# Preparing five Mambas' rates during attention, and moving small weight operations to ScalarE and GpSimd

## The chip, the cores and the metric

The kernel runs on one core of a Trainium2 chip, in one launch. The metric is the device time of that core in microseconds (us), the median of the runs shown; smaller is better.

## The reference, cut to what matters

Four layers work on an image `x` of 2 x 64 x 96 x 96 (batch, channels, height, width) in float32. Layer 0 is self-attention over the 9216 pixels of each image. Layer 1 is a depthwise and a pointwise convolution, then a Mamba over the pixels as one sequence. Layer 2 holds four Mambas: two (forward and backward) along one image axis, a linear map over both, then two along the other axis and a second linear map. Layer 3 makes a 3 x 3 filter from channel means and applies it. A Mamba, cut to its core:

```python
xz = einsum('nld,ed->nle', u, in_proj_w); x, z = split(xz, 2)
x = silu(conv1d(x, conv_w, causal, D_CONV=4) + conv_b)
dt, B, C = split(einsum('nld,ed->nle', x, x_proj_w), [4, 4 + 16])
dt = softplus(dt @ dt_proj_w.T + dt_proj_b)
A = -exp(A_log)                       # 128 channels x 16 states
h = exp(dt * A) * h + dt * B * x      # for each channel and state, step by step
y = (sum over states of h * C + x * Dp) * silu(z)
out = y @ out_proj_w.T
```

In layer 2 the input of each Mamba is normalised with a weight `norm_w`. What depends on the weights alone (A, the products of projections, repeats of rows for the layout) is worked out on the chip once for each Mamba; the change is about that preparation.

## The kernel before, in words

All of `x` stays in SBUF (`xa`, `xb`, 128 partitions: two images of 64 channels). Each engine takes its instructions in the order in which the program issues them; within the attention and the Mamba part that order is written out by hand.

**Attention** (`layer0_direct`). For each image b there are 18 blocks of 512 queries; each block has 18 steps n. A step issues eight score matmuls in 64-row pieces (L299), two exponentials (L313, ScalarE), two additions into a running sum (L402 and L411, VectorE) and the value matmuls of the step before (L324). At step 3 of a block the sums of the last block are made by a matmul into PSUM bank "m" (`sums`, L346) and inverted on VectorE (`invert`, L351 to L354). In image 0 each step ends with `next(ready_weights, None)`: one piece of the generator `prepare` (L1226), from one `yield` to the next. Its products also go to bank "m", of which there is one. `prepare` makes the tables, then everything of Mamba 0, in 16 pieces.

**Weights of a Mamba** (`mamba_weights`, L643). For Mamba i: A = -exp(A_log) (L649, L650); two products with the table `member` put A into place (L652) and a matmul turns that into `rates` (L658, copied at L661); for i > 0, `in_w` is multiplied by `norm_w` (L664); for each of four taps a matmul spreads the tap and a product with `in_w` stores it (L669, L671); then `low` (L675, L677), `step` (L679, L682), `direct`, the identity times D (L684), and in `by_state` (L631) four copies that repeat the rows of B and C (L639).

**Mamba part** (`layers1_2`, class `Mamba`). The work is cut into 120 units of 16 scan steps: 24 units of Mamba 0, whose scan state is carried on from unit to unit, then 96 units of Mambas 1 to 4, of whole sequences. A scan step is a decay on ScalarE (L973, exp), the input product `dt*x*B` on VectorE (L986), the scan on VectorE (L995 carried, L1000 whole), the product with C on GpSimd (L1002) and the gathering matmuls (L1013). The tables CARRY and FRESH give every event of a unit its due time in steps; `run` sorts all events of all units by time and issues them so. Most matmuls of this part, such as projections and weight products, share one double PSUM bank, "m".

The weights of Mambas 1 to 4 come in through the generator `other()`: two events of each carried unit, and two of each second whole unit, take one piece of it (`other_0`, `other_1`; due at 2.87 and 3.25, or at 0.72 and 0.40, steps after the unit begins). A product is issued in the first of two such pieces and read in the second. Such a pair is called a slot below. `other()` first finishes the pointwise convolution (7 slots), then takes for each of Mambas 1 and 2 7 slots, 4 for `joined` (L1276 on: the output weights multiplied with the linear map, with a fold of the identity's two halves at L1292), and the same for Mambas 3 and 4. The weights live in a part of `xa` handed out by a `Carver`; its first tiles are the scratch `placed` and the repeats of Mamba 0, made at the start of `layers1_2` on VectorE.

Of the kernel before, what the change touches and what calls it, by code (L numbers as in the profile page):

```python
# [25 lines left out]
P = 128  # L26
B, C, H, W = 2, 64, 96, 96
# [4 lines left out]
D_STATE, DT_RANK, D_CONV = 16, 4, 4  # L32
# [3 lines left out]
NMAMBA = 5  # L36


SPAN, BLOCKS, PARTS = 16, 8, 2
GROUP = P // SPAN  # L40
# [32 lines left out]
def rows_of(b):  # L73
    return slice(b * C, (b + 1) * C)
# [490 lines left out]
def products(nc, p, lhsT, rhs, m, n):  # L565

    each = lhsT if isinstance(lhsT, list) else [lhsT]
    for j, one in enumerate(each):
        nc.tensor.matmul(p[:m, j * n : (j + 1) * n], lhsT=one, rhs=rhs, start=True, stop=True)
    return p[:m, : len(each) * n]  # L570
# [25 lines left out]
def mamba_tables(k, pool):  # L596

    nc = k.nc  # L600
    t = SimpleNamespace()

    t.member = pool.tile([P, SPAN], FP, name="member")
    nc.vector.reduce_sum(t.member, k.ident.rearrange("p (b i) -> p i b", i=SPAN), axis=AX.X)
    t.block = pool.tile([P, 2, BLOCKS // 2], FP, name="block")
    for z in range(2):
        own = k.ident.rearrange("p (x z i) -> p z x i", z=2, i=SPAN)[:, z]
        nc.vector.reduce_sum(t.block[:, z], own, axis=AX.X)
    t.block = t.block.rearrange("p z x -> p (z x)")

    held = pool.tile([P, 3 * SPAN], FP, name="held")
    nc.vector.memset(held, 0.0)
    own = k.ident.rearrange("p (i g) -> p i g", g=GROUP)
    nc.vector.reduce_sum(held[:, SPAN : 2 * SPAN], own, axis=AX.X)
    t.gather = [held[:, SPAN:], held[:, :TILE]]

    t.centre = pool.tile([P, 2, C], FP, name="centre")
    for j in range(2):
        nc.vector.tensor_add(t.centre[:, j], k.ident[:, :C], k.ident[:, C:])
        nc.vector.tensor_scalar_add(t.centre[:, j], t.centre[:, j], -1.0 / C)  # L620
    t.centre = t.centre.rearrange("p j c -> p (j c)")
    return t


def scratch(k, t, pool):


    t.placed = pool.tile([P, PARTS, SPAN, GROUP], FP, name="placed")


def by_state(k, w, pool, i):  # L631

    x_w = k.mat(f"x_w{i}")
    w.bc = []
    for at in (DT_RANK, DT_RANK + D_STATE):
        bc = pool.tile([P, PARTS, SPAN, GROUP], FP, name=f"bc{i}_{at}")
        for j in range(PARTS):
            own = x_w[:, at + j * GROUP : at + (j + 1) * GROUP]
            k.nc.vector.tensor_copy(bc[:, j], own.unsqueeze(1).to_broadcast([P, SPAN, GROUP]))  # L639
        w.bc.append([bc[:, j].rearrange("p i g -> p (i g)") for j in range(PARTS)])  # L640


def mamba_weights(k, w, pool, product, tables, i):  # L643

    nc = k.nc
    a = pool.tile([P, D_STATE], FP, name=f"A{i}")
    nc.scalar.activation(a, k.col(f"A_log{i}"), AF.Exp)  # L649
    nc.vector.tensor_scalar_mul(a, a, -1.0)  # L650
    for j in range(PARTS):
        nc.vector.tensor_mul(  # L652
            tables.placed[:, j],
            tables.member.unsqueeze(2).to_broadcast([P, SPAN, GROUP]),
            a[:, j * GROUP : (j + 1) * GROUP].unsqueeze(1).to_broadcast([P, SPAN, GROUP]),
        )
    placed = [tables.placed[:, j].rearrange("p i g -> p (i g)") for j in range(PARTS)]
    p = product(placed, tables.block, P, BLOCKS)  # L658
    yield
    w.rates = pool.tile([P, PARTS, BLOCKS], FP, name=f"rates{i}")  # L660
    nc.vector.tensor_copy(w.rates.rearrange("p k b -> p (k b)"), p)  # L661
    in_w = k.mat(f"in_w{i}")
    if i:
        nc.vector.tensor_scalar_mul(in_w, in_w, k.col(f"norm_w{i}"))  # L664
    yield
    conv_w = k.col(f"convd_w{i}")
    w.taps = pool.tile([P, D_CONV, P], FP, name=f"taps{i}")
    for j in range(D_CONV):
        p = product(conv_w[:, j : j + 1].to_broadcast([P, P]), k.ident, P, P)  # L669
        yield  # L670
        nc.vector.tensor_mul(w.taps[:, j], in_w[:, :P], p)  # L671
        yield
    x_w = k.mat(f"x_w{i}")
    low = pool.tile([DT_RANK, P], FP, name=f"low{i}")
    p = product(x_w[:, :DT_RANK], k.ident, DT_RANK, P)  # L675
    yield
    nc.vector.tensor_copy(low, p)  # L677
    yield
    p = product(low, k.dtw(i), P, P)  # L679
    yield  # L680
    w.step = pool.tile([P, P], FP, name=f"step{i}")
    nc.vector.tensor_copy(w.step, p)  # L682
    w.direct = pool.tile([P, P], FP, name=f"direct{i}")
    nc.vector.tensor_scalar_mul(w.direct, k.ident, k.col(f"Dp{i}"))  # L684
    if i:
        by_state(k, w, pool, i)
    w.gate_w = in_w[:, P:]
    w.conv_b, w.dt_b = k.col(f"convd_b{i}"), k.col(f"dt_b{i}")
    w.out_w = k.mat(f"out_w{i}")
    yield  # L690


class Mamba:
# [35 lines left out]
    def product(self, lhsT, rhs, m, n):  # L729
        return products(self.nc, self.ps_m.tile([P, 2 * NB], FP, tag="m", name="mm"), lhsT, rhs, m, n)  # L730
# [495 lines left out]
def prepare(k, scratch_tile, product):  # L1226


    k.tables = mamba_tables(k, k.const)
    yield  # L1230
    scratch(k, k.tables, Carver(scratch_tile))
    yield
    k.weights = [SimpleNamespace() for _ in range(NMAMBA)]
    yield from mamba_weights(k, k.weights[0], k.const, product, k.tables, 0)


def layers1_2(k, pre, padded):
# [3 lines left out]
    nc, tc = k.nc, k.tc  # L1241
# [8 lines left out]
    with ExitStack() as stack:  # L1250
        m = Mamba(k, k.tables, *[stack.enter_context(p) for p in pools])
# [12 lines left out]


        carver = Carver(k.xa)
        scratch(k, k.tables, carver)
        by_state(k, k.weights[0], carver, 0)
        dtw = carver.tile([DT_RANK, (NMAMBA - 1) * P], FP)
        nc.sync.dma_start(out=dtw, in_=k.dtw_in[:, P:])  # L1270
        k.dtw = lambda i: dtw[:, bass.ts(i - 1, P)]

        def joined(which, lin_w, to):

            p = m.ps_m.tile([P, 2 * NB], FP, tag="m", name="mm")
            for d in range(2):
                lhsT = k.mat(f"out_w{which[d]}")
                nc.tensor.matmul(p[rows_of(d), :P], lhsT=lhsT, rhs=k.ident, start=True, stop=True)  # L1280
            yield
            turned = carver.tile([P, P], FP)
            nc.vector.tensor_copy(turned, p[:, :P])
            yield
            for d in range(2):
                p = m.product(turned[rows_of(d)], k.mat(lin_w, rows_of(d)), P, C)
                yield
                nc.vector.tensor_copy(to[d], p)
                yield
            fold = carver.tile([P, 2, C], FP)  # L1290
            for d in range(2):
                nc.vector.tensor_add(fold[:, d], k.ident[:, :C], k.ident[:, C:])  # L1292
            p = m.product(fold.rearrange("p a c -> p (a c)"), k.mat(lin_w), P, C)
            yield
            nc.vector.tensor_add(to[2], fold[:, 0], p)
            yield
# [6 lines left out]
        def other():  # L1303
            for c in range(FIRST, L // CH):
                part = k.xb[:, bass.ts(c, CH)]
                sides, whole = m.open()
                for j, p in enumerate(sides):
                    rhs = part[:, bass.ts(j, HALF)]
                    nc.tensor.matmul(p, lhsT=k.mat("conv_w"), rhs=rhs, start=True, stop=True)
                yield  # L1310
                nc.scalar.activation(part, whole, AF.Relu, bias=pre.bias, scale=pre.scale)
                yield
            for (which, lin_w, _), to in zip(layer2, joins):
                for i in which:
                    yield from mamba_weights(k, k.weights[i], carver, m.product, k.tables, i)
                yield from joined(which, lin_w, to)

        units = []
# [15 lines left out]
        for (which, _, lin_b), to, order in zip(layer2, joins, ("p (t n) -> p n t", "p (n t) -> p n t")):  # L1334
            xs = k.xb.rearrange(order, n=W)
            for b in range(B):
                rows = rows_of(b)
                for n in range(0, W, SEQS):
# [13 lines left out]
                    pair[1].last, norm.unit = pair, pair[0]  # L1352
                    units += pair
        m.run(units, first, FIRST, other(), padded.early)


# [134 lines left out]
@with_exitstack  # L1491
def conv_seq_kernel(ctx: ExitStack, tc: tile.TileContext, x, cols, mats, dtw, out):
    k = setup(ctx, tc, x, cols, mats, dtw)
    dram = ctx.enter_context(tc.tile_pool(name="dram", bufs=1, space=bass.MemoryType.DRAM))
    pre = Pre(k, dram)
    layer0(k, x, pre)
    padded = Padded(k)
    with tc.manual_schedule():
        layers1_2(k, pre, padded)
        layer3(k, padded, out)  # L1500
# [81 lines left out]
```

## Time and profile before

| what | us |
|---|---|
| median of 3 runs | 7395.57 (7389.34 to 7396.07) |
| profiled execution, its own time | 7391.99 |
| its span | 7389.9 |
| busy: TensorE, VectorE, ScalarE, GpSimd | 6327.8, 6725.5, 5478.5, 4613.1 |
| end of attention (VectorE writes `bad`) | 2389.6 |
| first scan of the Mamba part, last scan's end | 2452.2, 7332.3 |

The span is the time from the first to the last instruction in the profile; the rest of the execution's own time lies around it. Busy time is that of the engine's own work: waits don't count. TensorE's span of 2.4 ms at the beginning is attention, the rest mainly the 120 units.

### The profile page before, as it was taken

Reading aid. Unit: us, or ns where it says so; the run is one execution under the profiler, and the core shown is the slowest. Engines: PE = TensorE matmul, PEld = TensorE weight load, DVE = VectorE, ACT = ScalarE, POOL = GpSimd, SP = SyncE. Lnnn points to the kernel's source line nnn. Section 1 sums busy time; section 2 is a strip of 40 time slices with the busy share of each in tenths; the row PEclk is TensorE's granted clock in tenths of the full one; section 3 lists DMA queues with packets and bytes.
Section 4 is the critical chain, followed back from the end, with each engine's and each line's share of the span. In section 5 each row is a group of like instructions: output and inputs, shape, how many; then the busy total and the mean of one; then the engine's idle time right before and its main releaser. Section 6 shows DMA issues by size and latency. Waiting matters only on the chain. (4 is left out here: it accounts for less than half of the span.)

```text
span 7389.9 us, 106037 instructions
## 1 busy us (share of the span) xinstructions
PE 6327.8 (86%) x38502; PEld 2353.7 (32%) x38502; DVE 6725.5 (91%) x5732; ACT 5478.5 (74%) x7876; POOL 4613.1 (62%) x3074
## 2 busy tenths in 40 slices
PE   9999999999999788787788788788787777777777
PEld 3333333333333333222233233233233333333333
DVE  6787887888887599999999999999999999999999
ACT  5555555555555688787888888888888888888884
POOL 0000000000000498888899899999999999999996
PEclk9999999999999799998999999999999999999998
DMA  1000000000000466666667667667767676676764
GB/s 47 1 1 1 1 1 1 3 6 6 6 6 15 123 171 158 160 164 158 172 178 185 172 175 186 177 175 183 184 175 186 178 182 181 181 183 176 187 180 129
DMA packets 301155, 878.09 MB, mean 119 GB/s; under 512 B 33608, under 2 KB 35660, under 8 KB 300112
## 3 DMA queue, kind: packets, MB, share of 16 engines
q1 hardware_dynamic: 300184, 869.94, 45.3%
q8 instruction: 303, 4.96, 0.3%
q14 instruction: 228, 1.87, 0.1%
q10 hardware_dynamic: 440, 1.32, 0.1%
HBM read 767.71 MB, written 103.42 MB: 118 GB/s over the span
## 5 line engine op out<-in xcount | busy, mean ns | idle before, releaser
L1002 POOL TENSOR_TENSOR h<-h,C 128x768 f32<-128x768 f32 x1920 | 3457.0, 1821 | 308.8 <-DVE h L1000 257.2
L1000 DVE TENSOR_TENSOR_SCAN h<-h,place 128x768 f32<-128x768 f32 x1344 | 2285.9, 1736 | 13.3 <-ACT place L973 0.5
L313 ACT ACTIVATE e<-f_exp 128x1024 f32<-128x1024 f32 x1296 | 1258.0, 1022 | 986.5 <-PE f_exp L299 986.5
L986 DVE TENSOR_TENSOR place<-spread,B 128x768 f32<-128x768 f32 x1704 | 1545.4, 946 | 130.5 <-PE B L978 90.5
L973 ACT ACTIVATE h<-spread,xa 128x384 f32<-128x384 f32 x2688 | 1445.9, 605 | 8.5 <-DMA spread<-rows 7.1
L1013 PE MATMUL y<-h,held 128*32 128x384 f32 x7680 | 1105.5, 515 | 372.0 <-POOL h L1002 371.2
L324 PE MATMUL y<-e,xb 64*64 64x512 f32 x10368 | 1232.1, 590 | 0.0
L299 PE MATMUL f_exp<-theta,phi 64*64 64x512 f32 x10368 | 1230.0, 589 | 2.0 <-DVE xb L284 1.4
L402 DVE TENSOR_TENSOR acc_e<-acc_e,e 128x1024 f32<-128x1024 f32 x612 | 771.4, 1260 | 301.1 <-ACT e L313 283.4
L338 POOL TENSOR_TENSOR ys<-ys,y_one 128x512 f32<-128x512 f32 x36 | 46.0, 1277 | 1455.0 <-DVE ys L337 1455.0
L411 DVE TENSOR_TENSOR acc_e<-acc_e,e 128x1024 f32<-128x1024 f32 x612 | 811.0, 1325 | 65.9 <-DVE acc_e L402 2.8
L978 PE MATMUL B<-raw,xa 128*128 128x384 f32 x960 | 492.5, 598 | 269.9 <-DVE place L986 267.2
L995 DVE TENSOR_TENSOR_SCAN h<-h,state,place 128x384 f32<-128x384 f32 x720 | 670.6, 990 | 2.4
L324 PEld LDWEIGHTS y<-e,xb 64*64 64x64 f32 x10368 | 393.6, 133 | 728.1 <-issue 722.4
L299 PEld LDWEIGHTS f_exp<-theta,phi 64*64 64x64 f32 x10368 | 395.5, 133 | 715.0 <-issue 703.0
L1013 PEld LDWEIGHTS y<-h,held 128*32 128x32 f32 x7680 | 212.2, 109 | 1140.8 <-POOL h L1002 741.5
L363 POOL TENSOR_TENSOR xa<-xa,t_att 64x512 f32<-64x512 f32 x36 | 54.9, 1526 | 756.6 <-ACT t_att L361 736.0
L743 PE MATMUL mm<-dtu,ident 128*128 128x384 f32 x960 | 426.8, 550 | 26.8 <-ACT xb L1051 17.4
L920 PE MATMUL mm<-raw,xa 128*128 128x384 f32 x960 | 376.9, 516 | 29.9 <-ACT xn L781 27.0
L986 POOL TENSOR_TENSOR bx<-spread,xa 128x768 f32<-128x768 f32 x216 | 393.0, 1819 | 5.5 <-ACT xa L982 3.5
L973 ACT ACTIVATE h<-spread,rates 128x384 f32<-128x384 f32 x720 | 393.1, 606 | 3.5 <-DMA spread<-rows 2.9
L978 PEld LDWEIGHTS B<-raw,xa 128*128 128x128 f32 x960 | 159.4, 208 | 585.7 <-DVE place L986 419.2
(229 smaller groups left out, 7416.8 us busy)
## 6 DMA issues: line engine op xcount, KB each, us to landing
spread<-rows SPq DMA_DIRECT2D x1920, 384.0 KB, 6.1
rows<-dtu SPq DMA_DIRECT2D x120, 768.0 KB, 4.6
image<-pre SPq DMA_DIRECT2D x11, 384.0 KB, 2.3
xb<-image SPq DMA_DIRECT2D x11, 384.0 KB, 7.1
xa<-in_x SPq DMA_DIRECT2D x1, 2304.0 KB, 22.2
xa<-in_x SPq DMA_DIRECT2D x3, 384.0 KB, 11.6
xb<-in_x SPq DMA_DIRECT2D x3, 384.0 KB, 12.4
xa<-in_x SPq DMA_DIRECT2D x1, 1152.0 KB, 18.7
```

The lines of the kernel that those rows point to most:

```text
L299: nc.tensor.matmul(f[rows_of(half), bass.ts(side, NB)], lhsT=phi[at, m * P + half * C : m * P + (half + 1) * C], rhs=theta[at, bass.ts(i, ...
L313: nc.scalar.activation(e, f, AF.Exp)
L324: nc.tensor.matmul(ys[half][rows_of(side)], lhsT=g[at, m, :], rhs=e[at, bass.ts(side, NB)], start=m < 2, stop=m >= KEYS - 2,)
L402: nc.vector.tensor_add(block.acc, block.acc, es[0])
L411: nc.vector.tensor_add(block.acc, block.acc, es[1])
L973: self.nc.scalar.activation(u.decay[step][:, q], dt[:, q], AF.Exp, scale=rate)
L978: self.nc.tensor.matmul(self.B, lhsT=u.w.bc[0][part], rhs=x, start=True, stop=True)
L986: engine.tensor_mul(u.bx[step], self.spread(u, step, 1), B)
L995: nc.vector.tensor_tensor_scan(h[:, q], decay[:, q], bx[:, q], state[:, q : q + 1], ALU.mult, ALU.add)
L1000: nc.vector.tensor_tensor_scan(*flat, 0.0, ALU.mult, ALU.add)
L1002: nc.gpsimd.tensor_mul(h, h, C)
L1013: self.nc.tensor.matmul(y, lhsT=self.t.gather[block // 4], rhs=u.h[step][:, q], start=False, stop=stop)
```

## The change

It has five parts.

1. `mamba_weights` is split. A new `mamba_rates` holds A, the placing products, `rates` and the scaling of `in_w` by `norm_w`. `prepare` calls it for all five Mambas, in attention, before the rest of Mamba 0's weights; it has one `yield` more, between the placing products and their matmul. The pieces of `prepare` go from 16 to 26.
2. Taps are made two to a product: two matmuls into one PSUM tile, then two multiplications, so two slots a Mamba in place of four.
3. The repeats of B and C go from VectorE to ScalarE, and `by_state` yields after each pair of copies, so for Mambas 1 to 4 they have a slot of their own after `step`. For Mamba 0 all four are issued at the start of `layers1_2`.
4. `direct` goes from VectorE to ScalarE.
5. The two fold sums of `joined` go from VectorE to GpSimd.

The scratch `placed` is no longer carved from `xa` in `layers1_2`. A Mamba takes 5 slots of `other()` in place of 7.

```diff
@@ by_state
-            k.nc.vector.tensor_copy(bc[:, j], own.unsqueeze(1).to_broadcast([P, SPAN, GROUP]))
+            k.nc.scalar.copy(bc[:, j], own.unsqueeze(1).to_broadcast([P, SPAN, GROUP]))
         w.bc.append([bc[:, j].rearrange("p i g -> p (i g)") for j in range(PARTS)])
-def mamba_weights(k, w, pool, product, tables, i):
+        yield
+def mamba_rates(k, w, pool, product, tables, i):
...
     placed = [tables.placed[:, j].rearrange("p i g -> p (i g)") for j in range(PARTS)]
+    yield
     p = product(placed, tables.block, P, BLOCKS)
     yield
     w.rates = pool.tile([P, PARTS, BLOCKS], FP, name=f"rates{i}")
     nc.vector.tensor_copy(w.rates.rearrange("p k b -> p (k b)"), p)
-    in_w = k.mat(f"in_w{i}")
     if i:
+        in_w = k.mat(f"in_w{i}")
         nc.vector.tensor_scalar_mul(in_w, in_w, k.col(f"norm_w{i}"))
     yield
+def mamba_weights(k, w, pool, product, i):
+    nc = k.nc
+    in_w = k.mat(f"in_w{i}")
     conv_w = k.col(f"convd_w{i}")
     w.taps = pool.tile([P, D_CONV, P], FP, name=f"taps{i}")
-    for j in range(D_CONV):
-        p = product(conv_w[:, j : j + 1].to_broadcast([P, P]), k.ident, P, P)
+    for j in range(0, D_CONV, 2):
+        p = product([conv_w[:, j + n : j + n + 1].to_broadcast([P, P]) for n in range(2)], k.ident, P, P)
         yield
-        nc.vector.tensor_mul(w.taps[:, j], in_w[:, :P], p)
+        for n in range(2):
+            nc.vector.tensor_mul(w.taps[:, j + n], in_w[:, :P], p[:, bass.ts(n, P)])
         yield
...
-    nc.vector.tensor_scalar_mul(w.direct, k.ident, k.col(f"Dp{i}"))
-    if i:
-        by_state(k, w, pool, i)
+    nc.scalar.mul(w.direct, k.ident, k.col(f"Dp{i}"))
...
     yield
+    if i:
+        yield from by_state(k, w, pool, i)
@@ prepare
-    yield from mamba_weights(k, k.weights[0], k.const, product, k.tables, 0)
+    for i in range(NMAMBA):
+        yield from mamba_rates(k, k.weights[i], k.const, product, k.tables, i)
+    yield from mamba_weights(k, k.weights[0], k.const, product, 0)
@@ layers1_2
-        scratch(k, k.tables, carver)
-        by_state(k, k.weights[0], carver, 0)
+        for _ in by_state(k, k.weights[0], carver, 0):
+            pass
...
-                nc.vector.tensor_add(fold[:, d], k.ident[:, :C], k.ident[:, C:])
+                nc.gpsimd.tensor_add(fold[:, d], k.ident[:, :C], k.ident[:, C:])
...
-                    yield from mamba_weights(k, k.weights[i], carver, m.product, k.tables, i)
+                    yield from mamba_weights(k, k.weights[i], carver, m.product, i)
```

## The prediction

> **What bounds the kernel now.** I read the page first, then the busy time of engines by windows, the timelines of VectorE and TensorE around the edited lines, and last the groups of instructions.
>
> ```profile
> PE 6327.8 (86%) x38502; PEld 2353.7 (32%) x38502; DVE 6725.5 (91%) x5732; ACT 5478.5 (74%) x7876; POOL 4613.1 (62%) x3074
> DVE  6787887888887599999999999999999999999999
> ```
>
> The kernel has two regimes. Up to about 2394 us it is attention, where TensorE works without gaps and VectorE has room. From 2452 us to 7332 us the 120 Mamba units run and VectorE is full. Busy time by windows inside that part:
>
> ```profile
> core 0: us, PE busy (x) PEld busy (x) DVE busy (x) ACT busy (x) POOL busy (x), PEclk, DMA share, GB/s
> 2661.00:2745.00 84.00, 70.89 (x290) 25.92 (x290) 83.79 (x95) 72.38 (x112) 76.33 (x75) 0.96 0.66 169
> 5451.00:5765.00 314.00, 249.11 (x1062) 97.24 (x1058) 309.43 (x241) 268.94 (x428) 291.98 (x173) 0.96 0.70 181
> ```
>
> VectorE is idle 0.2 of 84 us and 4.6 of 314 us, ScalarE 14% in both: a microsecond taken from VectorE here should come off the span. Now VectorE where a weight step falls (columns: start, time of the row, engine, line, operation, count, idle time before and what ended it):
>
> ```profile
> 2792.35 1.92 DVE L995 TENSOR_TENSOR_SCAN h<-h,state,place 128x384 f32<-128x384 f32 x2
> 2795.72 0.18 DVE L650 TENSOR_SCALAR xa<-xa 128x16 f32<-128x16 f32 x1 [1.45 <-ACT xa L649]
> 2795.93 2.11 DVE L652 TENSOR_TENSOR xa<-member,xa 128x128 f32<-128x128 f32 x2
> 2798.73 0.17 DVE L661 COPY xa<-mm 128x16 f32<-128x16 f32 x1 [0.69 <-PE mm L569]
> 2798.82 1.03 DVE L664 TENSOR_SCALAR mats<-mats,cols 128x256 f32<-128x256 f32 x1
> 2799.78 1.91 DVE L995 TENSOR_TENSOR_SCAN h<-place,state,bx 128x384 f32<-128x384 f32 x2
> ...
> 3057.44 0.29 DVE L682 COPY xa<-mm 128x128 f32<-128x128 f32 x1 [0.52 <-PE mm L569]
> 3057.65 0.94 DVE L684 TENSOR_SCALAR xa<-ident,cols 128x128 f32<-128x128 f32 x1
> 3058.52 3.88 DVE L639 COPY xa<-mats 128x128 f32<-128x128 f32 x4
> 3062.31 1.91 DVE L995 TENSOR_TENSOR_SCAN h<-place,state,bx 128x384 f32<-128x384 f32 x2
> ```
>
> The scans stand still from 2794.2 to 2799.8 for the rates and from 3056.9 to 3062.3 for step, direct and repeats: 5.5 us each time, though the operations are tiny. The four copies of L639 take 0.21 us when nothing is in the way and up to 1.85, the length of one GpSimd product (L1002, 1.82).
>
> **What the Trainium skill says.** "SBUF — State Buffer", Who interferes with whom: a VectorE copy or tensor_scalar in a two-port mode, or a product of two SBUF inputs, and a GpSimd operation hold one port pair as a lock for the whole instruction, and ScalarE never waits for it. The spread of L639, L652 and L684 fits; the ScalarE half is not tested by any row here. "Perfetto Trace Analysis", Optimizing Scalar/DVE Operations: with VectorE saturated, moving work to ScalarE may pay, to GpSimd perhaps not, because of that pair. For prices, "ScalarE: Activation LUTs", What ACT_TABLE_LOAD costs: 186 ns + 0.833 per element, 93 more for a pointer operand.
>
> **The change in the Mamba part.** From the starts of the first scan of each unit in VectorE's timeline I take unit lengths. In the first 24 units (scans carried on) an undisturbed one, units 4 to 6, takes 42.12 us; from unit 60 on a pair takes 38.79 + 39.68 = 78.47. Whatever is above is what the weight slots cost, whatever engine makes it.
>
> Carried part, units 7 to 22, excess in order: rates 5.64; four tap slots 1.23, 1.81, 0.50, 0.48; low 0.29; step with direct and repeats 5.49. Second Mamba: 5.63; 1.40, 0.49, 0.49, 0.50; 0.28; 5.50. Join: 2.50, 0.38. Sum 32.6. After it:
> - No rates slot. Two tap slots, each with two products (0.85 instead of 0.49 us of TensorE by L569) and two L671 (0.29 more): 0.5 + 0.35 + 0.29, so 1.1 each.
> - low 0.3. Step keeps its L682 alone: 0.5. Two slots of two repeats on ScalarE: 2 x 0.29 by the page's price; bounded by the 0.20 of L649 (16 wide) and 0.48 of L1017 (384 wide). `direct`, with a pointer, 0.39. All queue in ScalarE ahead of decays that are needed two to three steps (about 8 us) later; cover is ScalarE's 14% idle. I count 0.3 per Mamba; without cover it would be 1.5.
> - That is 3.3 per Mamba, 6.6 for two.
> - The join moves up into units 17 to 20: 1.5, 0.4, 0.4 and the fold slot. There GpSimd's sums (0.28 each: L1002 is 1.82 at 768 wide, the least L342 1.26 at 512, so 2.2 ns per element and 0.14) stand behind state copy 0.19 and product 1.81 of the scan just done; TensorE's product (0.65), with the matmuls queued behind it, and VectorE's add (0.22), with the next scan behind it, wait: 3.4 in all, from 2.5 if GpSimd is early to 6 if it lags.
> - Taps of the third Mamba, units 21 and 22: 2.6.
>
> Sum 14.9: **17.7 saved**. The slot at the end of unit 23 is 3542.11 to 3546.44, a fold with its lock; afterwards a step copy of 0.8: **3.5 saved**.
>
> Free part, units 24 to 59: 1434.5 us against 18 x 78.47 = 1412.5, so 22.0 above, almost all in two rates slots, two repeats slots with the pair after, and the fold of unit 59 (2.4). After it: passage into this part 1.0, repeats 0.3, two tap slots 0.6 each (single ones were hidden in the 0.9 us that odd units idle anyway), the rest of Mamba 4 0.2, join -0.5, fold 2.7 (as in the timeline at 4978 us, where GpSimd ends the previous product only at 4980.0). Sum 4.9: **17.1 saved**. Mamba part: 38.3, between 28 and 45 as slots recover less or more.
>
> **The change in attention.** Every added matmul lies on the full engine. TensorE, then VectorE of the second block:
>
> ```profile
> 49.28 0.61 PE L569 MATMUL m<-block,scratch 128*128 128x8 f32 x4 [2.19 <-DVE scratch L652]
> 56.85 0.49 PE L569 MATMUL m<-ident,cols 128*128 128x128 f32 x2
> ...
> 116.86 1.13 PE L346 MATMUL m<-fold,ones 128*128 128x512 f32 x2
> 117.92 1.95 PE L324 MATMUL y<-e,xb 64*64 64x512 f32 x16
> ...
> 119.67 3.35 DVE L351 RECIPROCAL inv<-m 128x512 f32<-128x512 f32 x1
> 124.45 0.69 DVE L354 SCALAR_TENSOR_TENSOR ok<-m,ok 128x512 f32<-128x512 f32 x1
> ```
>
> Rates now yield between L652 and the product, so the 2.2 wait goes; four more products of 0.55 come: +2.2 - 2.3 = -0.1. VectorE's added 0.7 to 1.0 per rates fits its 0.7 to 1.5 of idle per step. But preparation grows from 16 steps to 26, past the block's 18. Counting them, the product of `low` falls on step 3 of the second block, right behind `sums`, and needs the same PSUM bank "m", which VectorE reads until L354 ends at 125.1, now about 126.3. TensorE, in order, would reach it at about 120.6: **5.7 lost**, with all scores behind it. `sums` itself waits 0.4 for the tap products. Attention +6.0; if VectorE catches up sooner +3, if each rates product stalls too +10.
>
> At the passage the four repeats of Mamba 0 go to ScalarE, which idles 10.43 us before L208 at 2400.70; they start when depthwise has freed `xa` (2398.9) and take 1.2: nothing, up to 1 us if they are dearer. No DMA is moved; SP keeps its order.
>
> Sum: 6.0 - 38.3 = -32.3. The profiled execution has 7392.0 (span 7389.9 and 2.1 around it), so 7359.7. The median of the runs shown is 3.6 higher; I say 7361.
>
> **Rivals.** (1) As above, 7361, chance 0.76. (2) VectorE's time is given back in the free part: GpSimd is busy 292 of 314 there and may be the next limit, so only the carried part and unit 23 pay: 7392.0 + 6.0 - 21.2 = 7377. For it: taps in the free part already cost nothing. Against: the stops there show in the units' lengths. Chance 0.10. (3) Slower: the free part's units alternate 38.79 and 39.7, and the 0.8 us of the odd ones ends on ScalarE's copy of B (L982), so ScalarE is just in time at the unit's edge. If the moved work leaves it late for good and both units take 39.7, all 48 pairs pay 0.9: +43 - 32 = +11, 7403. It decides from 0.7 us per pair. Against it: after every disturbance (units 38, 52, 84) the old rhythm comes back within a pair or two, and the moved work is over by unit 45. Chance 0.07. (4) Attention at +10, both folds at 6 us and half the free gain: 7392.0 + 10 - (38.3 - 6 - 8.5) = 7378, 7382 on the footing of the median, which is within 0.2% (15 us, about what a measurement of this kernel can tell from no change). Chance 0.07.
>
> Range 7348 to 7378: the low end takes 45 saved and attention at +3 or so, the high end rival 2. Chances: faster 0.86, same 0.07, slower 0.07.
>
> **What would show it.** Right: L650 to L664 only before 110 us and at 0.17 to 0.35 each; no VectorE row for the repeats, `direct` or the fold; units 7 to 22 near 43 us, none at 47; one TensorE wait of 5 to 6 us near 121 us; the last scan about 32 us earlier. Wrong: unit lengths from unit 60 on other than 78.47 per pair, ScalarE repeats above 0.5 us, or a fold slot of over 6 us.

## The result, and the profile after

The changed kernel takes 7365.94 us (median of 6 runs, 7363.2 to 7369.59), against 7395.82 (6 runs, 7389.34 to 7400.15) before: 29.9 us less, a ratio of 0.996 with a 95% interval of 0.9948 to 0.9973. The forecast was 7361, 34.6 under the median that it stood on. The profiled execution took 7363.2 with a span of 7361.4, which is 28.5 under the span before; the working had said 32.3.

The page of the changed kernel, its busy times and VectorE's row over the span:

```profile
PE 6309.5 (86%) x38502; PEld 2346.8 (32%) x38502; DVE 6694.1 (91%) x5703; ACT 5493.7 (75%) x7902; POOL 4609.6 (63%) x3078
DVE  6878777888888499999999999999999999999999
```

VectorE lost 31.4 us of busy time and 29 instructions, ScalarE gained 15.2, and the span fell by nearly what VectorE lost. Busy time by windows, in the same two places of the Mamba part as before:

```profile
core 0: us, PE busy (x) PEld busy (x) DVE busy (x) ACT busy (x) POOL busy (x), PEclk, DMA share, GB/s
2669.00:2753.00 84.00, 70.56 (x290) 25.66 (x288) 83.79 (x95) 72.26 (x113) 76.25 (x75) 0.96 0.66 168
5423.00:5737.00 314.00, 249.15 (x1060) 96.88 (x1056) 309.53 (x241) 269.60 (x428) 291.84 (x173) 0.96 0.70 181
```

Where no weights are prepared nothing changed: VectorE is as full, and the other engines stand to it as before. The difference must lie in the slots and in attention. The slot with `step`, on VectorE's timeline, which before had stopped the scans for 5.5 us:

```profile
2929.29 1.92 DVE L1005 TENSOR_TENSOR_SCAN h<-h,state,place 128x384 f32<-128x384 f32 x2
2931.38 0.29 DVE L692 COPY xa<-mm 128x128 f32<-128x128 f32 x1 [0.18 <-PE mm L569]
2931.59 1.92 DVE L1005 TENSOR_TENSOR_SCAN h<-place,state,bx 128x384 f32<-128x384 f32 x2
```

The scan before it ends at 2931.2 (the row begins at 2929.29 and lasts 1.92) and the next begins at 2931.6: 0.4 us are left of 5.5. The rows of the moved operations, by their lines (count, then least, median and longest duration in ns, then the first and last start):

```profile
L650 DVE TENSOR_SCALAR A<-A x5: 168/169/171, 47.9 to 91.3; 128x16 f32<-128x16 f32 x5
L665 DVE TENSOR_SCALAR mats<-mats,cols x4: 345/345/347, 65.9 to 98.9; 128x256 f32<-128x256 f32 x4
L639 ACT COPY xa<-mats x20: 284/296/299, 2400.1 to 4008.5; 128x128 f32<-128x128 f32 x20
L694 ACT ACTIVATE xa<-ident,cols x4: 390/390/393, 2932.4 to 3929.5; 128x128 f32<-128x128 f32 x4
```

All five Mambas' rates are done by 99.3 us, and both of these VectorE operations run at their bare length, with no spread. On ScalarE every one of the twenty repeats takes 0.28 to 0.30, every `direct` 0.39: no spread, where VectorE's copies had gone from 0.21 to 1.85, and near the 0.29 and 0.39 that the working had priced them at.

The price in attention, on TensorE's timeline of the second block:

```profile
115.84 1.95 PE L324 MATMUL y<-e,xb 64*64 64x512 f32 x16
123.12 0.59 PE L569 MATMUL m<-ident,mats 128*4 128x128 f32 x2 [5.33 <-DVE ok L354]
123.64 3.35 PE L299 MATMUL f_exp<-theta,phi 64*64 64x512 f32 x16
126.82 1.89 PE L324 MATMUL y<-e,xb 64*64 64x512 f32 x16
```

TensorE stands for 5.3 us behind the inversion, as forecast. What the forecast did not have is the next row: sixteen score matmuls that take 1.90 elsewhere take 3.35. Busy time by windows shows a lower granted clock over the same time (it follows the busy times):

```profile
110.00:120.00 10.00, 7.79 (x66) 2.30 (x58) 9.10 (x8) 3.88 (x4) 0.40 (x1) 1.00 0.00 0
120.00:125.00 5.00, 1.88 (x10) 0.65 (x14) 2.93 (x4) 0.00 (x0) 0.00 (x0) 0.81 0.01 3
125.00:130.00 5.00, 5.00 (x44) 1.64 (x40) 2.64 (x3) 2.41 (x3) 0.00 (x0) 0.85 0.00 0
130.00:140.00 10.00, 10.00 (x84) 3.17 (x80) 6.51 (x7) 6.42 (x8) 0.24 (x1) 1.00 0.01 2
```

The clock falls with the pause and is back a few microseconds later.

For all that follows, the span is cut into stages by starts of rows in the timelines: attention from the first score matmul to the flag `bad`; the passage from there to the first scan; then the units by the starts of their first scans. Units 7 to 22 hold the weight slots of the carried part, 25 to 59 those of the free part. "From sums to sums" is the time from the second block's `sums` matmul to the third's. "The fold unit" is the one whose slot makes the fold sums: in the changed kernel unit 20 of the carried part, and unit 43, taken with its neighbour 44, in the free part. Each experiment was timed once, the two kernels of the last one five times; every row of the table is one profile.

| kernel | attention | sums to sums | units 0-6 | 7-22 | 23-24 | 25-59 | 60-119 |
|---|---|---|---|---|---|---|---|
| before | 2352.8 | 64.2 | 335.5 | 706.5 | 92.0 | 1394.7 | 2351.5 |
| changed | 2359.6 | 72.2 | 333.8 | 694.3 | 89.3 | 1376.0 | 2351.0 |
| again | 2360.6 | 73.5 | 333.9 | 690.5 | 89.4 | 1375.6 | 2351.6 |
| undo_rates | 2349.1 | 64.2 | 336.6 | 705.3 | 90.9 | 1379.8 | 2351.6 |
| undo_repeats | 2359.6 | 72.2 | 336.6 | 702.5 | 87.1 | 1383.9 | 2350.7 |
| undo_fold | 2360.6 | 73.4 | 336.4 | 688.7 | 84.1 | 1376.0 | 2351.6 |
| undo_taps | 2359.4 | 72.0 | 335.7 | 685.2 | 91.3 | 1374.8 | 2352.4 |
| fix_bank | 2351.7 | 65.2 | 339.5 | 696.6 | 84.1 | 1375.9 | 2351.6 |
| fold_table | 2360.6 | 73.4 | 336.1 | 688.4 | 88.5 | 1371.9 | 2351.7 |
| pad_slots | 2359.4 | 72.0 | 336.2 | 685.0 | 87.8 | 1375.0 | 2352.4 |
| all_three | 2352.6 | 65.2 | 333.3 | 686.5 | 90.7 | 1372.5 | 2351.2 |
| fix_fold_pad | 2352.0 | 65.2 | 335.6 | 685.9 | 90.7 | 1372.4 | 2351.5 |

From before to changed: attention +6.9 in itself, the start and the passage +0.7, units 0 to 6 -1.7, 7 to 22 -12.2, 23 and 24 -2.7, 25 to 59 -18.7, the rest -0.7; with these roundings -28.4 of the span's -28.5.

### The profile page after: what moved, and what is told of

Same layout as the page of the kernel before. It is cut to its first block, busy times and chain, and to the rows that moved or that the text cites. A ratio compares the mean times of both kernels' runs of the same rounds, so it can differ in the third digit from the quotient of the medians.

```text
span 7361.4 us, 106021 instructions
## 1 busy us (share of the span) xinstructions
PE 6309.5 (86%) x38502; PEld 2346.8 (32%) x38502; DVE 6694.1 (91%) x5703; ACT 5493.7 (75%) x7902; POOL 4609.6 (63%) x3078
## 4 chain that ended last, share of the span: by engine, by line
DVE 16%; issue 13%; PE 11%; ACT 6%; POOL 4%; DMA 2%; DVEq 0%; POOLq 0%; SPq 0%; ACTq 0%
DVE h L1010 9%; DVE place L996 7%; PE mm L753 6%; POOL h L1012 3%; DMA spread<-rows 2%; ACT h L983 2%; PE conv L855 2%; PE y L1023 1%; PE B L988 1%; PE y L1018 1%; ACT raw L860 1%; ACT raw L866 0%; DVE done L1483 0%; ACT xa L817 0%; ACT raw L869 0%
## 5 line engine op out<-in xcount | busy, mean ns | idle before, releaser
L1012 POOL TENSOR_TENSOR h<-h,C 128x768 f32<-128x768 f32 x1920 | 3454.1, 1819 | 291.0 <-DVE h L1010 240.7
L983 ACT ACTIVATE h<-spread,rates 128x384 f32<-128x384 f32 x3408 | 1845.3, 608 | 8.6 <-DMA spread<-rows 6.9
L299 PEld LDWEIGHTS f_exp<-theta,phi 64*64 64x64 f32 x10368 | 395.5, 133 | 714.6 <-issue 702.5
L930 PE MATMUL mm<-raw,xa 128*128 128x384 f32 x960 | 380.0, 520 | 29.9 <-ACT xn L791 27.6
L1010 DVE TENSOR_TENSOR_SCAN h<-place,bx 128x768 f32<-128x768 f32 x192 | 334.0, 1739 | 0.3 <-ACT place L983 0.3
```

Source lines behind the costliest of these rows:

```text
L299: nc.tensor.matmul(f[rows_of(half), bass.ts(side, NB)], lhsT=phi[at, m * P + half * C : m * P + (half + 1) * C], rhs=theta[at, bass.ts(i, ...
L983: self.nc.scalar.activation(u.decay[step][:, q], dt[:, q], AF.Exp, scale=rate)
L1010: nc.vector.tensor_tensor_scan(*flat, 0.0, ALU.mult, ALU.add)
L1012: nc.gpsimd.tensor_mul(h, h, C)
```

## The experiments

My theory: in the Mamba part VectorE sets the pace, and a slot costs the time for which it stops VectorE, whichever engine makes it wait; moving an operation pays where it shortens that stop. The rival readings were that the number of slots is what counts, that GpSimd takes back what VectorE gains, and that an offload helps whatever it is waited for by. Each experiment starts from the changed kernel.

**The same kernel again.** No edit.

> The changed kernel once more, to see how much of a difference between two profiles is the kernel's and how much the execution's. If the units' lengths are as fixed as the free part's rhythm suggests, the fold unit is 47.3 us again, the carried units 7 to 22 sum to 694 within 1 us, and the span from the first scan to the last is within 2 us of 4844. If executions differ in how TensorE and ScalarE stand to VectorE, the units after a tap slot (8, 9, 13) move by a microsecond and the sum by 3 to 5. The wait for bank m is 5.3 us again, and the matmuls behind it run at a lower clock for some 2 to 3 us, as in the four runs with it so far.

It took 7365.15. The carried fold unit is 47.8 (47.3 in the first profile), the Mamba part from first scan to last 4841.0 against 4844.4. The difference sits in single units with tap slots or just after them: unit 8 is 43.0 in place of 44.3, unit 9 42.4 for 43.7, unit 13 43.1 for 44.3, and unit 10 43.9 for 42.6. So the second reading held: two profiles of one kernel differ by 3.8 us in units 7 to 22, and smaller differences there say nothing. Units 4 to 6, ahead of every weight slot, repeat to 0.02 us; late in the free part single ones differ by up to 0.8.

**Rates back in the Mamba part.**

```diff
-    for i in range(NMAMBA):
-        yield from mamba_rates(k, k.weights[i], k.const, product, k.tables, i)
+    yield from mamba_rates(k, k.weights[0], k.const, product, k.tables, 0)
...
+                    yield from mamba_rates(k, k.weights[i], k.const, m.product, k.tables, i)
                     yield from mamba_weights(k, k.weights[i], carver, m.product, i)
```

> The changed kernel with the rates and the norm scaling of Mambas 1 to 4 put back into the Mamba part (one more slot each, as before the change); only Mamba 0's stay in attention. My theory (VectorE bounds the Mamba part, and a rates slot stops its scans for some 5.5 us): attention ends 7.5 us earlier than in the changed kernel (four products of 0.55 go, and the wait for bank m of 5.3 goes since preparation ends inside the first block); two carried units grow to 47.7 us (+11); two free pairs grow by 4 to 6 (+9); the third Mamba's taps move into the free part (-4). In all +8 to +9. Rival (the gain came from having fewer slots, or VectorE's time is given back in the free part): the units stay near 43 and 78.5 a pair, and the kernel is 5 to 8 us faster than the changed one.

The `yield` that the change added stays for Mamba 0 alone, and the scratch `placed` is carved in `layers1_2` again. It took 7373.61; the span is 10.1 longer than the changed kernel's. Units 7 and 13, with the rates, are 47.73 us each, and units 7 to 22 are 11.0 longer; the third Mamba's rates fall into unit 23 (51.3 for 46.8), the fourth's into unit 33 (44.1 for 39.2), and units 25 to 59 are 3.8 longer; attention is 10.5 shorter, where 7.5 had been said. That the folds move too, to units 22 (48.1) and 51 (42.0), makes the sum less clean than its parts. The rival, 5 to 8 us faster, is out: the rates slots cost VectorE 5.6 us each in the carried part. From first scan to last this kernel takes 19.8 us more than the changed one, of the 35.8 by which the change shortened that part; but 10.5 of them come back in attention, so that moving the rates is worth about 10 of the 28.5 us of the span, less than the repeats below.

**Repeats and direct back on VectorE.**

```diff
-            k.nc.scalar.copy(bc[:, j], own.unsqueeze(1).to_broadcast([P, SPAN, GROUP]))
+            k.nc.vector.tensor_copy(bc[:, j], own.unsqueeze(1).to_broadcast([P, SPAN, GROUP]))
...
-    nc.scalar.mul(w.direct, k.ident, k.col(f"Dp{i}"))
+    nc.vector.tensor_scalar_mul(w.direct, k.ident, k.col(f"Dp{i}"))
```

> The changed kernel with the repeats of B and C and direct back on VectorE, slots unchanged. My theory (VectorE is full and these operations stand behind GpSimd's hold on the shared port pair): each of the copies takes 0.2 or about 1.85 us, direct 0.9 to 1.3; a carried Mamba costs about 5 us more, a free one 2.5: +15 in all. Rival (the engine does not matter, only that the copies have a slot of their own): less than +3.

It took 7379.82, 14 more than the changed kernel (span 16.6 more). The rows of the repeats, and a slot of them on the timelines of VectorE and GpSimd in this kernel (rows between left out):

```profile
L639 DVE COPY xa<-mats x20: 213/220/1850, 2404.6 to 4026.3; 128x128 f32<-128x128 f32 x20
```

```profile
2973.82 1.92 DVE L1005 TENSOR_TENSOR_SCAN h<-h,state,place 128x384 f32<-128x384 f32 x2
2975.52 1.81 POOL L1012 TENSOR_TENSOR h<-h,C 128x768 f32<-128x768 f32 x1
2975.65 3.79 DVE L639 COPY xa<-mats 128x128 f32<-128x128 f32 x4
2977.54 1.82 POOL L1012 TENSOR_TENSOR h<-h,C 128x768 f32<-128x768 f32 x1
2979.36 1.91 DVE L1005 TENSOR_TENSOR_SCAN h<-place,state,bx 128x384 f32<-128x384 f32 x2
```

Four copies of 0.21 us by their least length hold VectorE for 3.8 between two scans, and the whole unit (number 11) is 45.86 where the changed kernel has 42.14. Units 7 to 22 are 8.2 longer, 25 to 59 7.9. The same work on ScalarE costs nothing that the units show. The theory held in mechanism: eight of the twenty copies are long (1.76 to 1.85), and each of the eight ends 0.08 to 0.09 us after a product of GpSimd, here after the ends of L1012 at 2977.3 and 2979.4. In size it held for the carried Mambas (about 5 us each); the two free ones cost 4.0 each where 2.5 was expected. The port pair that the Trainium skill's "SBUF — State Buffer" (Who interferes with whom) describes fits the two lengths, 0.21 and 1.85, and ScalarE's single one of 0.28 to 0.30 fits its sentence that ScalarE doesn't wait there.

**Fold sums back on VectorE.**

```diff
-                nc.gpsimd.tensor_add(fold[:, d], k.ident[:, :C], k.ident[:, C:])
+                nc.vector.tensor_add(fold[:, d], k.ident[:, :C], k.ident[:, C:])
```

> The changed kernel with the fold sums back on VectorE. My theory (in both places TensorE's product and then VectorE's add wait for the sums; on VectorE they wait for GpSimd's hold on the port pair, on GpSimd for its queue): the carried fold unit goes from 47.3 to about 46.7 and the free one stays within 0.5 us of 42.0; the whole within 1 us. Rival (moving the sums to GpSimd was a gain, as the engine table suggests): both fold units grow by 1.5 to 3 us, +3 to +6 in all.

Neither came. It took 7357.28 in its one run. The carried fold unit is 44.75 in place of 47.3 to 47.8; the free one with its neighbour is 82.2 in place of 81.6. This is the carried slot of the changed kernel, all engines by the timeline (rows between left out):

```profile
3356.30 1.92 DVE L1005 TENSOR_TENSOR_SCAN h<-h,state,place 128x384 f32<-128x384 f32 x2
3357.99 1.80 POOL L1012 TENSOR_TENSOR h<-h,C 128x768 f32<-128x768 f32 x1
3360.00 1.80 POOL L1012 TENSOR_TENSOR h<-h,C 128x768 f32<-128x768 f32 x1
3361.77 0.59 POOL L1304 TENSOR_TENSOR xa<-ident 128x64 f32<-128x64 f32 x2
3362.41 0.69 PE L569 MATMUL mm<-mats,xa 128*128 128x64 f32 x2 [4.47 <-POOL xa L1304]
3363.14 0.22 DVE L1307 TENSOR_TENSOR xa<-xa,mm 128x64 f32<-128x64 f32 x1 [4.92 <-PE mm L569]
```

and this the same slot with the sums on VectorE:

```profile
3358.34 1.92 DVE L1005 TENSOR_TENSOR_SCAN h<-h,state,place 128x384 f32<-128x384 f32 x2
3360.01 1.81 POOL L1012 TENSOR_TENSOR h<-h,C 128x768 f32<-128x768 f32 x1
3360.17 1.87 DVE L1304 TENSOR_TENSOR xa<-ident 128x64 f32<-128x64 f32 x2
3362.18 0.41 PE L569 MATMUL mm<-mats,xa 128*128 128x64 f32 x2 [1.08 <-ACT h L983]
3362.63 0.22 DVE L1307 TENSOR_TENSOR xa<-xa,mm 128x64 f32<-128x64 f32 x1 [0.59 <-PE mm L569]
```

On GpSimd the two sums take 0.59 but come after two queued products, since GpSimd is one scan step behind; TensorE waits 4.5 and VectorE 4.9 for them. On VectorE they wait once, until the product of GpSimd beside them ends (3361.8), and are done 1.8 us after the scan (3362.0). My working had one product in front, and its doubt about a move to GpSimd was the port pair; what cost here is GpSimd's queue. In this slot the offload to GpSimd costs 2.6 to 3.0 us; in the free part it gains 0.6. The rest of the 7.7 us between the two Mamba parts is in units 8, 9 and 13, which vary without any edit, and in units 23 and 24; these give 5.2, but they read 84.1 in fix_bank too, where the sums are on GpSimd, so that this isn't shown to be the edit's.

**Taps one to a product.**

```diff
-    for j in range(0, D_CONV, 2):
+    taken = 1 if i else 2
+    for j in range(0, D_CONV, taken):
```

The two inner loops run over `range(taken)`.

> The changed kernel with the taps of Mambas 1 to 4 one to a product again (four tap slots each; Mamba 0 in attention keeps two). My theory (VectorE pays for the products, not for the slots, and a slot with two products makes it wait longer): four single slots with the unit after cost 3 to 4 us per carried Mamba, where the two double ones with the unit after cost 3.4 to 4.7; and the third Mamba's taps move out of the carried part, where they cost 4.7, into the free part, where single taps cost nothing: 4 to 6 us faster than the changed kernel. Rival (fewer slots are the gain): 2 to 4 us slower.

It took 7363.08. First scan to last is 5.0 shorter than in the first profile of the changed kernel, as expected, but only 1.6 shorter than in the second, and not at the place that was expected. Unit 20 gives 5.2 of it (42.13 for 47.3), because the join, pushed back by four slots, no longer has its fold there; units 23 and 24, where the fold now falls, are only 2.0 longer. Units 7 to 19 take 555.9, against 558.1 and 556.0 in the two profiles of the changed kernel: eight single tap slots (0.5 to 1.8 us each) cost what four double ones (0.9 to 2.4) do. And units 21 and 22 are 87.2 with the join's products in place of the third Mamba's taps, 88.9 and 86.8 in the two profiles. So the rival's 2 to 4 us slower is out, and my reason, the third Mamba's taps, isn't shown either: the one clear difference is at the fold.

**Empty slots.** Four more `yield`s after each Mamba's weights:

```diff
                     yield from mamba_weights(k, k.weights[i], carver, m.product, i)
+                    for _ in range(4):
+                        yield
```

> The changed kernel with two empty slots after each of Mambas 1 to 4, so that the third Mamba's taps leave the carried part again and the number of slots is that of before the change. My theory (a slot costs what is in it; nothing is lost with more of them): empty units at 42.12, the third Mamba's taps nearly free in the free part: 3 to 6 us shorter from the first scan to the last. Rival (fewer slots are worth something by themselves): no gain, or slower.

It took 7358.45; first scan to last is 4836.5, 7.9 and 4.5 less than in the two profiles of the changed kernel. Units 12, 13, 19 and 20, whose slots are empty, read 42.12 to 42.13. So a slot as such costs nothing, and fewer of them are worth nothing. Here too the gain is in unit 20, which lost the fold (5.2), while units 7 to 19 take 555.4; units 21 and 22 hold the join at 43.9 and 43.7, and the third Mamba's taps, now in units 25 and 27, read 39.35 and 39.46, within the 38.8 to 39.7 of units without.

**A free bank in attention.**

```diff
+    if i == 0:
+        yield
+        yield
     p = product(x_w[:, :DT_RANK], k.ident, DT_RANK, P)
```

> The changed kernel with two empty pieces ahead of the product of low in attention, so that it no longer falls on the step whose sums and inversion hold bank m. My theory (TensorE is the full engine there and its stop is lost for good, with a lower clock after it): the wait of 5.3 us is gone, the first block after it runs at 1.9 us per 16 matmuls, and attention from the second block's sums to its end is 6.5 to 8 us shorter; the Mamba part is as in the changed kernel. Rival (the block has slack elsewhere, and VectorE, which is behind at that point, catches up in the pause): attention shortens by less than 2 us, since TensorE then waits for VectorE later.

It took 7361.89. TensorE's timeline over the place of the wait in this kernel:

```profile
118.33 1.95 PE L324 MATMUL y<-e,xb 64*64 64x512 f32 x16
120.10 1.90 PE L299 MATMUL f_exp<-theta,phi 64*64 64x512 f32 x16
121.82 1.90 PE L324 MATMUL y<-e,xb 64*64 64x512 f32 x16
```

No pause and no slow rows; from sums to sums it is 65.2 us in place of 72.2 and 73.5, and attention 7.9 to 8.9 shorter. The seven profiles with the pause have 72.0 to 73.5 there; it thus cost 6.8 to 8.3, not its own 5.3, and nothing of it was made up later. The Mamba part was 3.3 longer than in the changed kernel: its filling units 0 to 6 took 339.5 where other runs have 333 to 337. all_three, with the same edit, has 333.3 there, so that loss is not the edit's in every execution; what sets it is not settled.

**Fold sums from the tables.** They are made once in `mamba_tables`, where half of that sum was computed anyway, and `joined` takes them from there.

```diff
+    t.fold = pool.tile([P, 2, C], FP, name="fold")
     for j in range(2):
-        nc.vector.tensor_add(t.centre[:, j], k.ident[:, :C], k.ident[:, C:])
-        nc.vector.tensor_scalar_add(t.centre[:, j], t.centre[:, j], -1.0 / C)
+        nc.vector.tensor_add(t.fold[:, j], k.ident[:, :C], k.ident[:, C:])
+        nc.vector.tensor_scalar_add(t.centre[:, j], t.fold[:, j], -1.0 / C)
...
-            fold = carver.tile([P, 2, C], FP)
-            for d in range(2):
-                nc.gpsimd.tensor_add(fold[:, d], k.ident[:, :C], k.ident[:, C:])
+            fold = k.tables.fold
```

> The changed kernel with the fold sums made once, with the tables in attention, and none in the join. My theory (TensorE's product, and behind it VectorE's add, wait for GpSimd's queue): the carried fold unit falls from 47.3 to about 42.6 us, the free one with its neighbour from 81.6 to about 78.6; 7 to 8 us in all. If the wait were TensorE's own backlog (it reads its operands late because of the matmuls before it), the carried unit would stay above 46.

It took 7357.85. The carried fold unit is 42.50, the free one 39.89 with 38.80 after it: 4.8 and 2.9 less, 7.7 together. VectorE's timeline of the slot:

```profile
3360.91 1.92 DVE L1006 TENSOR_TENSOR_SCAN h<-h,state,place 128x384 f32<-128x384 f32 x2
3362.96 0.22 DVE L1306 TENSOR_TENSOR xa<-fold,mm 128x64 f32<-128x64 f32 x1
3363.09 1.92 DVE L1006 TENSOR_TENSOR_SCAN h<-place,state,bx 128x384 f32<-128x384 f32 x2
```

The product itself leaves no wait that the view lists, and TensorE's own backlog is out as a cause. The wait for GpSimd, its two queued products and the sums, was the price.

**Together.** all_three joins the free bank, the fold from the tables and single taps; fix_fold_pad has double taps and the empty slots in place of single taps.

> The changed kernel with three of the edits together: two empty pieces ahead of low in attention, the fold sums from the tables, and the taps of Mambas 1 to 4 one to a product in four slots. My theory (the three costs lie at different places and add up): attention from the second block's sums to its end is 2272.8 us again, 8 to 9 us less than in the changed kernel; no unit between 7 and 22 is above 44.7; from the first scan to the last 4828 to 4836; in all 7340 to 7350 us, against 7366 for the changed kernel. Rival (what is freed at one place is taken back at the next, as the fill of the first units took back part of the gain with the free bank): 7355 to 7360.

> The same, but with the taps two to a product as in the changed kernel and two empty slots after each Mamba in place of two more tap slots. If a slot with two products costs VectorE more than two slots with one (1.0 to 2.2 us, and the unit after it up to 1.5), this is 1 to 3 us slower than the version with single taps; if only the place of the third Mamba's taps matters, the two are equal within 1 us: both 7340 to 7350 us.

In five runs each they took 7347.74 (7346.47 to 7352.03) and 7349.08 (7346.35 to 7353.01), against 7395.51 of the kernel before in 9 runs: a ratio of 0.9937 for both (0.9923 to 0.9950, and 0.9923 to 0.9951). That is 18 and 17 us less than the six runs of the changed kernel; the 1.3 us between the two lie within the spread of their runs. The stages of all_three show two gains side by side: attention 7.0 shorter than in the changed kernel, and the fold slots, with unit 20 at 42.14 and units 43 and 44 at 78.5. Fold and bank alone had given 7.7 and 7.9 to 8.9, about 16; the spans differ by 16.7. First scan to last is 4834.2 and 4836.1, and 4836.6 in fold_table, which has neither single taps nor empty slots: once the fold is gone, how many taps go to a product and in which slots they lie can't be told apart.

## Why the prediction was right, and where its sizes were off

**The bound.** Right. VectorE's busy time fell by 31.4 and the span by 28.5, and the units from 60 on stayed at 78.4 a pair. Rival 2, GpSimd giving the gain back in the free part, is refuted: units 25 to 59, where it would have shown, gave the largest share, 18.7. Rival 3, a rhythm in which ScalarE stays late, didn't appear: units 60 to 119 take 2351.0 against 2351.5. Rival 4 needed attention at +10, both fold units at 6 us over and half the free gain; attention lost 6.9, the fold units were 5.2 and 3.1 over, and units 24 to 59 saved 15.9 of 17.1. Taken back one at a time, the parts of the change move the span by +10.1 (rates), +16.6 (repeats and `direct`), -6.2 (fold sums) and -0.4 (taps). So two parts make the gain, the fold sums took some of it back, and pairing the taps gave nothing that can be told from the 3.8 us between two profiles of one kernel. The four add up to 20 of 28.5: each is one execution, and each edit also shifts the slots behind it.

**The sum.** 32.3 was worked out and 28.5 came. Part of this closeness is luck: units 0 to 6 gave 1.7 and unit 23 gave 2.0 that were not worked out, in units that vary by more than that over the kernels run here; without them the sum would be off by 7.5. The forecast isn't its own sum either: 7359.7 and the 3.6 up to the median make 7363.3, and the text went to 7361 without a reason. The median was 7365.94.

**Free part.** Units 24 to 59 saved 15.9 where 17.1 was worked out. The fold was put at 2.7: unit 43 with its neighbour is 3.1 over a pair. The passage into this part was put at 1.0 and is 3.7 (unit 24 at 42.47); what makes units 23 and 24 so variable, 84 to 92 us over all runs, stays open.

**Carried part.** Here the term was mis-sized: units 7 to 22 saved 12.2 in the profile after (16.0 in the second profile) where 17.7 was worked out; the sign "none at 47" failed at unit 20, with 47.3. Two items. The fold slot was put at 3.4 and is 5.2: I counted one GpSimd product ahead of the sums, there were two; the text had this as its upper end ("6 if it lags"). Double tap slots were put at 1.1 and are 0.9 to 2.4 (single ones, too, reach 1.8 in undo_taps): whether TensorE's product is just in time or a microsecond late for VectorE differs from one execution to the next (in unit 8 VectorE waits 1.67 us for it in the profile after and 0.41 in the second one). The working took 0.5 for a slot, as five of the eight tap slots before show, and left out the other three, at 1.23 to 1.81. With the units behind them, the taps of three Mambas are 5.2 over what was worked out in the profile after, more than the fold's 1.8, and the repeats and the other slots of the join give 1.5 back; in the second profile the taps, with the `step` slots, are only some 1.0 over. Repeats were put at 0.3 a Mamba and cost 0.02. Unit 23 saved 5.5 for 3.5.

**Attention.** +6.0 was worked out, and attention became 6.9 longer. The wait for bank "m" was placed to its step and sized 5.7; it is 5.33. The matmuls cost less than nothing: without the wait, in fix_bank and the two joint kernels, attention takes 2351.7 to 2352.6 against 2352.8 before, where -0.1 and 0.4 for `sums` had been worked out. One reason is visible: two tap matrices in one product take 0.71, not twice 0.49. What was missing is the clock after the pause: wait and clock together take 7.0 of the 8.0 us that the block lost from sums to sums (72.2 against 65.2 in fix_bank, 64.2 before); that `low` and `step`, which came into this block from the first, take the rest is inferred. (Counted by `yield`s, the pieces of `prepare` go from 16 to 25, not 26; the step of `low` stays the same.)

**Passage.** 0 to 1 was worked out for the repeats of Mamba 0: the text had them start once the depthwise convolution frees `xa`, but they ran from 2400.14, before it began (2400.24). The first activation was not held by them: it comes 6.4 us after that beginning, and 6.5 before. From the flag to the first scan it is 62.5 before and 64.1 after, but 62.8 to 65.7 in the other runs with the same edit, and 64.7 in undo_repeats without it, so no size can be given to it.

## What to carry to other kernels

On a full engine, price a small operation by the gap that it leaves between the engine's regular rows, not by its own length: here a copy of 0.2 us could hold VectorE for 1.85, and a slot of some 1.2 us of work by bare lengths stood for 5.5. An operation moved to another engine brings that engine's queue with it: free if nobody waits for it soon (ScalarE's repeats), dearer than before if a product waits at once (GpSimd's fold), and gone if the result can be made once, earlier. When preparation is stretched over a loop that shares a PSUM bank, count its pieces against the loop's own use of the bank; two empty pieces were worth 7 to 9 us of attention here.

## What the runs showed of the hardware that was not expected

The pause of TensorE cost more than itself. After the 5.33 us wait in attention, the next sixteen 64-row matmuls took 3.09 to 3.69 us in the seven profiles with that wait, in place of 1.90, and in three of these the sixteen after them still took 2.72 to 2.90. Windows of undo_fold over the pause, after which the clock was lowest:

```profile
120.00:125.00 5.00, 0.00 (x0) 0.00 (x0) 4.82 (x4) 0.00 (x0) 0.00 (x0) 0.88 0.00 0
125.00:130.00 5.00, 4.99 (x26) 1.53 (x30) 1.23 (x1) 1.74 (x2) 0.00 (x0) 0.50 0.02 3
130.00:140.00 10.00, 10.00 (x94) 3.41 (x90) 6.05 (x6) 4.47 (x6) 0.00 (x0) 0.97 0.00 0
```

In the 5 us window in which TensorE works again its granted clock is 0.50; in the next it is 0.97. From what length of pause on it happens, the runs don't show.
